# Where the convolution weights and a second image's rows are asked for, and seven early units instead of eight

## The chip, the cores and the metric

One core of one Trainium2 chip. The metric is the device time of one execution in microseconds (us); less is better. The kernel before took 3022.46 us, the median of 3 runs (3018.35 to 3022.87). Everything is float32.

## What is computed

Two layers on x of shape (2, 256, 64, 64). Layer 0: attention over all 4096 pixels with 8 heads of 32 channels, a 1x1 convolution of x and its result, blended with x by a mask. Layer 1: a channel gate, attention in windows of 8 x 8 pixels, and then the part that the change is about:

```
x = x + o                                     # o: window attention
x = channel shuffle in 4 groups
y = conv 7x7, 64 groups of 4 channels -> 64   # sa_w1
y = relu(batch norm 1(y))
y = conv 7x7, 64 groups, 64 -> 256            # sa_w2
return x * sigmoid(batch norm 2(y))
```

## The kernel before

**Stages.** Projections q, k, v of all pixels go to DRAM (to about 187 us of the span). Then one loop over 512 slots (image, chunk of 512 pixels, half of the heads, piece of 128 keys) does layer 0's attention, to about 2781 us. The rest of layer 0 and the window attention of a finished chunk are the steps of a generator (`stage`), laid between the slots. Each chunk ends in a store of 8 image rows into a DRAM tensor `xs` (line 979). The last chunk of image 1 comes through after the loop, between 2784 and 2850 us, so the last rows of image 1 are in `xs` only then. All of image 0 is there much earlier.

**The convolutions** (`convolve`, a generator, from line 992) come last. They are written as matmuls with banded weights: a band covers 30 rows of a padded column block, three blocks make the 64 rows, so a unit of 16 channels (4 groups of 4) for one image is 3 x 64 = 192 moving columns, and for both images 384. There are 16 units. The loop runs over *items*, each a unit and the images it is done for:

```
items = [(u, (0,)) for u in range(EARLY)] + [(u, (1,)) for u in range(2, EARLY)]
items += [(u, (0, 1)) for u in range(EARLY, NU)] + [(1, (1,)), (0, (1,))]
```

With EARLY = 8 that is items 0 to 7 for image 0 (units 0 to 7), items 8 to 13 for image 1 (units 2 to 7), items 14 to 21 for both (units 8 to 15), and 22 and 23, units 1 and 0 of image 1: 24 items. A single item is one without, a pair one with both images.

**One item k.** `conv1` (matmuls on line 1045 into PSUM tile c1a, ReLU by ScalarE on line 1053 into yca), then `conv2` (matmuls on line 1069 into two PSUM tiles c2a, tanh on line 1079 and a scaling on line 1085 by ScalarE into tile za, of which there are two), then `gate` (a product by VectorE on line 1091, and 12 stores for each image to the output, line 1104). In program order conv1 of item k + 1 goes ahead of conv2 of item k. The stores go to the queues of GpSimd (POOL) and SyncE (SP) in turn; those of image 0's items that come after the last chunk is through go to GpSimd alone (line 1096).

**Loads**, all on SyncE's queue, which runs in program order:
- `load_w(u)`, line 1017: one unit's two weight bands, 128 partitions x 1792 values, 896 KB, in the profile wa<-ws. Unit 0 has a buffer of its own; the others take the buffers (8 of them, EB) in which attention kept its exponentials ea, so a first load into one waits until VectorE has added up the exponentials there, and a ninth load waits for the unit that was there before. Units come from a list `weights`: 1 to 15, then 1 again for item 22.
- `load_x(k)`, line 1024: the rows of item k, 128 x 3 x 280 values, 420 KB for each image. Image 0's early items take four buffers xea, later ones four buffers xla. `load_rows(n)` issues these loads up to item n, and stops at items of image 1 until the last chunk is through (`staged`). The first xla loads are then issued by `more()`, four at once; since they read `xs`, they wait until the store of the last rows has landed. For the last chunk two of these four stores are on SyncE's queue and two on GpSimd's.

**Order around the change.** Two weights (units 1 and 2) are asked for at attention's end; after the gate of each of the items 0 to 6 one more; after item 7 none; from item 8 on one per item. After the loop of slots a step of the convolution generator alternates by hand with steps of `stage` for the last chunk (lines 1199 to 1210). SyncE's queue thus holds, from attention's end: w1, w2; stores of item 0, rows of item 4, w3; stores of 1, rows of 5, w4; stores of 2, rows of 6, w5; stores of 3, rows of 7, w6; the store of the last rows; rows of items 8 to 11; w7, w8, w9; stores of item 8, rows of 12, w10; and so on.

TensorE's order there is: conv1 of items 0 and 1, the last chunk's steps with conv1 of item 2 to 5 and conv2 of items 0 to 3 between them, the last projection (line 953, opa), conv2 of item 4, conv1 of 6, conv2 of 5, conv1 of 7, conv2 of 6, conv1 of 8.

Of the kernel before, what the change touches and what calls it, by code (L numbers as in the profile page):

```python
# [29 lines left out]
AHEAD = 2  # L30
EB = 8
DN = 8
EARLY = 8
HEADS1, HD1 = 4, 64
WS = 8
NW = W // WS
# [19 lines left out]
def conv_seq_kernel(ctx: ExitStack, tc: tile.TileContext, a, out):  # L56
# [467 lines left out]
    def pipeline(arm, shifted, pools):  # L524
# [462 lines left out]

        items = [(u, (0,)) for u in range(EARLY)] + [(u, (1,)) for u in range(2, EARLY)]
        items += [(u, (0, 1)) for u in range(EARLY, NU)] + [(1, (1,)), (0, (1,))]
        staged = []  # L990

        def convolve():
# [12 lines left out]
            weights = deque([*range(1, NU), 1])  # L1005
            dst = out.rearrange("b (g i) r w -> b i r g w", i=4)

            def load_w(u):
                if u >= NU:
                    return  # L1010
                n = 2 * 32 * UW
                if u == 0:
                    t = cpool.tile([P, n], F32, name=f"w{arm}{u}")
                else:
                    t = ep.tile([P, HG, CH], F32, tag="e", name=f"w{arm}{u}")
                    t = t.rearrange("p h n -> p (h n)")[:, 0:n]
                nc.sync.dma_start(t, w_s[u])
                ws[u] = t

            def load_x(k):  # L1020
                u, images = items[k]
                x = xs[k] = early[k % 4] if k < EARLY else xcs[k % 4]
                for i, b in enumerate(images):
# [5 lines left out]
            def load_rows(k):  # L1029

                while len(xs) < min(k + 1, len(items)) and (
                    staged or B - 1 not in items[len(xs)][1]
                ):
                    load_x(len(xs))

            def conv1(k):
                if k >= len(items):
                    return
                u, images = items[k]
                n = nb * len(images)  # L1040
                w = ws[u][:, 0 : 32 * UW].rearrange("p (m g d) -> p g d m", g=UG, d=KS)
                s = psum1(f"c1{arm}{k}")
                for d in range(KS):
                    for j in range(4):
                        nc.tensor.matmul(  # L1045
                            s[32 * j : 32 * j + 32, 0 : n * W],
                            w[:, j, d, :],
                            xs[k][:, 0:n, j, d : d + W],
                            start=(d == 0),
                            stop=(d == KS - 1),  # L1050
                        )
                y = ys[k] = ycs[k % 2]
                nc.scalar.activation(
                    y[:, 0:n, PAD : PAD + W],
                    s[:, 0 : n * W].rearrange("p (n x) -> p n x", x=W),
                    AF.Relu,
                    bias=cbias1[:, u : u + 1],
                )

            def conv2(k):  # L1060
                u, images = items[k]
                n = nb * len(images)
                y = ys.pop(k)
                w = ws[u][:, 32 * UW :].rearrange("p (m d) -> p d m", d=KS)
                tiles = [psum2(f"c2{arm}{k}_{hh}") for hh in range(2)]
                for d in range(KS):
                    for j in range(4):
                        r = slice(32 * j, 32 * j + 32)
                        nc.tensor.matmul(  # L1069
                            tiles[j // 2][:, j % 2, 0 : n * W],  # L1070
                            w[r, d],
                            y[r, 0:n, d : d + W],
                            start=(d == 0),
                            stop=(d == KS - 1),
                        )
                z = pool.tile([P, 4, B * nb * W], F32, tag="z", name=f"z{arm}{k}", bufs=2)
                z = z[:, :, 0 : n * W]
                for hh in range(2):
                    nc.scalar.activation(  # L1079
                        z[:, 2 * hh : 2 * hh + 2, :],  # L1080
                        tiles[hh][:, :, 0 : n * W],
                        AF.Tanh,
                        scale=0.5,
                    )
                nc.scalar.activation(z, z, AF.Copy, bias=0.25, scale=0.25)
                return z.rearrange("p j (n x) -> p j n x", x=W)

            def gate(k, z):
                u, images = items[k]
                x = xs[k][:, 0 : nb * len(images), :, PAD : PAD + W]  # L1090
                nc.vector.tensor_mul(z, z, x.rearrange("p n g x -> p g n x"))  # L1091

                engines = (nc.gpsimd, nc.sync)
                if k == len(items) - 1:
                    engines = (nc.scalar, nc.sync)
                elif staged and k < EARLY:
                    engines = (nc.gpsimd,)
                stores = 0
                for m, b in enumerate(images):
                    for n, (x0, r0, r1) in enumerate(BLOCKS):  # L1100
                        for i in range(4):
                            p = 32 * i + 1 - x0
                            stores += 1
                            engines[stores % len(engines)].dma_start(  # L1104
                                dst[b, i, r0:r1, UG * u : UG * u + UG, :],
                                z[p + r0 : p + r1, :, nb * m + n, :],
                            )


            def more():  # L1110
                if staged and not xcs:

                    for n in range(3):
                        t = ep.tile([P, HG, CH], F32, tag="sum", name=f"xl{arm}{n}", bufs=3)
                        t = t.rearrange("p h n -> p (h n)")[:, 0 : B * nb * UG * WP]
                        xcs.append(t.rearrange("p (n g w) -> p n g w", n=B * nb, g=UG, w=WP))
                    xcs.append(pool.tile([P, B * nb, UG, WP], F32, name=f"xl{arm}3"))
                    load_rows(EARLY + 3)
                return bool(xcs)
# [2 lines left out]
            load_rows(3)  # L1122
            load_w(0)
            pool = yield
            for _ in range(2):
                load_w(weights.popleft())
            conv1(0)
            yield
            for k, (u, images) in enumerate(items):
                while len(xs) <= k + 1 < len(items):  # L1130
                    if not more():
                        yield
                conv1(k + 1)
                yield
                more()
                z = conv2(k)
                yield
                more()
                gate(k, z)
                if xcs or k + 4 < EARLY:  # L1140
                    load_rows(k + 4)

                if weights and (k < EARLY - 1 or k >= EARLY):
                    load_w(weights.popleft())

        def run_later():
# [23 lines left out]
        for i, (b, c, g, m) in enumerate(slots):  # L1170
            now[0] = i
            if (b, c, g, m) == (B - 1, NCHUNK - 1, 0, 0):
                for _ in banded:
                    pass
                conv = convolve()
                next(conv)
            if m % PB == 0:
                load_piece(i // PB + AHEAD)
            if g == KC - 1 and m == 0:
                nxt = (b, c + 1) if c + 1 < NCHUNK else (b + 1, 0)  # L1180
                if nxt[0] < B:
                    load_q(*nxt)
            rest = scores(i + 2) if i + 2 < len(slots) else None
            products(i)
            if rest:
                rest()
            if g == KC - 1 and m == NMB - 1:
                at(DN + 6, lambda b=b, c=c: stages.append(stage(b, c)))
            run_later()
            if i % 5 == 1:  # L1190
                next(banded, None)
            if i % 4 == 0:
                run_stages()
# [102 lines left out]
```

## Time and profile before

| | |
|---|---|
| median of 3 runs | 3022.46 us (3018.35 to 3022.87) |
| the profiled execution, its own time | 3021.93 us |
| its span, first to last instruction | 3020.1 us |
| TensorE (PE) busy | 2970.8 us, 98% |
| VectorE (DVE), ScalarE (ACT) busy | 2503.1 us, 2480.6 us |
| GpSimd (POOL) busy | 267.1 us |
| mean granted TensorE clock | 0.993 |

By stretches of the span (us):

| stretch | length | TensorE busy | clock | GB/s |
|---|---|---|---|---|
| attention, 140 to 2781 | 2641.0 | 2630.3 | 1.00 | 76 |
| last chunk and items 0 to 3, 2781.0 to 2847.3 | 66.3 | 61.3 | 0.97 | 101 |
| items 4 to 13, 2847.3 to 2910.2 | 62.9 | 53.4 | 0.92 | 179 |
| pairs and the end, 2910.2 to 3020.1 | 109.9 | 93.9 | 0.93 | 155 |

How to read the lines that follow. Times are from the span's start. A line of a timeline or of the chain has start, length, engine, source line, and output<-inputs of a group of instructions. "SPq" is SyncE's queue, where a DMA's issue stands, not its transfer. "x56" counts the matmul records of a group. In brackets is the time for which the engine was idle before, and what released it. The chain of waits is the work that ended last, followed back from the end.

### The profile page before, as it was taken

How to read it: one execution, taken by the hardware profiler on the slowest of the kernel's cores; microseconds unless marked ns; L12 is line 12 of the kernel's file. 1: busy time of each engine (PE TensorE's matmuls, PEld its weight loads, DVE VectorE, ACT ScalarE, POOL GpSimd, SP SyncE). 2: the span in 40 equal slices, each digit the busy share in tenths (PEclk: the TensorE clock that was granted, in tenths of full speed). 3: DMA queues.
4: the chain of work that ended last, by engine and by line, in shares of the span. 5: the costliest groups of instructions: out<-in, count | busy, mean ns of one | idle time of the engine just before them, and what ended most of it. 6: DMA issues, size and time to landing. Idle time of an engine off the chain costs nothing.

```text
span 3020.1 us, 61026 instructions
## 1 busy us (share of the span) xinstructions
PE 2970.8 (98%) x25226; PEld 1017.2 (34%) x25226; DVE 2503.1 (83%) x1348; ACT 2480.6 (82%) x4151; POOL 267.1 (9%) x470
## 2 busy tenths in 40 slices
PE   9999899999999999999999999999999999999897
PEld 3552223223222222222223222323223222323585
DVE  3249989999999999998999999999999998998211
ACT  5569789898989898988989898989898998988333
POOL 8010000000000000000000000000000000000456
PEclk9999999999999999999999999999999999999998
DMA  8544322222142323232222222222323222321564
GB/s 243 196 174 160 107 69 66 69 65 70 52 80 63 79 62 73 66 73 68 67 68 64 71 58 67 62 73 62 80 59 69 71 71 67 104 60 54 163 196 104
DMA packets 224143, 266.03 MB, mean 88 GB/s; under 512 B 113576, under 2 KB 130300, under 8 KB 223600
## 3 DMA queue, kind: packets, MB, share of 16 engines
q1 hardware_dynamic: 200880, 231.47, 26.2%
q0 software_dynamic: 18416, 27.87, 4.4%
q8 instruction: 201, 3.29, 0.5%
q10 hardware_dynamic: 4560, 2.70, 0.3%
q14 instruction: 86, 0.70, 0.1%
HBM read 213.49 MB, written 66.13 MB: 93 GB/s over the span
## 4 chain that ended last, share of the span: by engine, by line
PE 92%; DVE 2%; DMA 2%; POOL 1%; ACT 1%; issue 1%; SPq 0%; ACTq 0%; DVEq 0%; POOLq 0%
PE sa L633 36%; PE ava L662 33%; PE hya L732 4%; PE qka L803 4%; PE vwa L889 2%; PE opa L953 2%; PE v L472 2%; PE q L435 2%; PE k L435 2%; DVE suma L664 1%; POOL out_dram L1104 1%; PE c1a L1045 1%; PE c2a L1069 1%; DMA out_dram<-za 1%; PE dna L685 1%
## 5 line engine op out<-in xcount | busy, mean ns | idle before, releaser
L664 DVE TENSOR_TENSOR suma<-suma,ea 128x2048 f32<-128x2048 f32 x960 | 2199.1, 2291 | 88.7 <-ACT ea L643 2.3
L643 ACT ACTIVATE ea<-sa 128x512 f32<-128x512 f32 (+1 forms) x3072 | 2044.8, 745 | 86.6 <-PE sa L633 39.3
L633 PE MATMUL sa<-qa,ka 32*128 32x512 f32 x8192 | 1191.4, 640 | 1.5 <-ACT vst L480 1.2
L662 PE MATMUL ava<-ea,va 128*32 128x512 f32 x8192 | 1091.6, 605 | 0.3 <-ACT fa L672 0.3
L633 PEld LDWEIGHTS sa<-qa,ka 32*128 32x128 f32 x8192 | 338.0, 183 | 755.4 <-ACT ea L643 688.3
L662 PEld LDWEIGHTS ava<-ea,va 128*32 128x32 f32 x8192 | 161.5, 108 | 779.7 <-issue 752.9
L979 POOL DMA_DIRECT2D xs<-xo x94 | 65.8, 708 | 2552.0 <-DVE xo L964 2551.8
L1104 POOL DMA_DIRECT2D out_dram<-za x210 | 117.9, 569 | 85.0 <-DVE za L1091 61.1
L803 PE MATMUL qka<-ua,qkv_w 128*128 128x512 f32 x256 | 118.4, 605 | 0.0
L664 DVE TENSOR_TENSOR suma<-ea,ea 128x2048 f32<-128x2048 f32 x32 | 73.1, 2284 | 51.3 <-ACT ea L643 51.3
L1091 DVE TENSOR_TENSOR za<-za,xla 128x768 f32<-128x768 f32 (+1 forms) x16 | 21.7, 1359 | 108.0 <-DMA out_dram<-za 57.9
L454 DVE TENSOR_REDUCE top<-sq 128x512 f32<-128x2048 f32 x16 | 36.6, 2286 | 81.3 <-ACT sq L448 81.3
L1069 PE MATMUL c2a<-yca,wa 32*128 32x192 f32 (+1 forms) x1344 | 98.1, 435 | 2.5 <-ACT za L1079 2.5
L740 ACT ACTIVATE ta<-hya,bf 128x512 f32<-128x512 f32 x32 | 20.2, 683 | 96.8 <-PE hya L732 96.8
L1079 ACT ACTIVATE za<-c2a 128x384 f32<-128x384 f32 (+1 forms) x48 | 26.1, 595 | 86.5 <-DMA out_dram<-za 61.4
L1069 PEld LDWEIGHTS c2a<-yca,wa 32*128 32x128 f32 x1344 | 89.6, 315 | 13.1 <-issue 9.8
L858 ACT ACTIVATE ewa<-ewa,mxwa 128x64 f32<-128x64 f32 x256 | 85.2, 346 | 1.5 <-DVE mxwa L849 1.5
L744 DVE TENSOR_TENSOR ta<-ta,mca 128x512 f32<-128x512 f32 x32 | 22.0, 689 | 67.6 <-ACT ta L740 67.6
L816 ACT ACTIVATE qka<-qka,qkv_b 128x512 f32<-128x512 f32 x64 | 40.4, 683 | 41.8 <-PE qka L803 41.6
L803 PEld LDWEIGHTS qka<-ua,qkv_w 128*128 128x128 f32 x256 | 46.0, 189 | 71.3 <-issue 46.1
L435 PE MATMUL q<-x,WqT 128*128 128x512 f32 x128 | 61.3, 624 | 5.6 <-DMA WqT<-in_WqT_dram 5.6
L889 PE MATMUL vwa<-qkv_w,ua 128*128 128x256 f32 x256 | 59.5, 386 | 0.0
(137 smaller groups left out, 1523.5 us busy)
## 6 DMA issues: line engine op xcount, KB each, us to landing
ka<-ks SPq DMA_DIRECT2D x256, 256.0 KB
va<-vs SPq DMA_DIRECT2D x256, 256.0 KB
wa<-ws SPq DMA_DIRECT2D x17, 896.0 KB
ws<-zeros SPq DMA_DIRECT2D x16, 896.0 KB
xs<-xo POOLq DMA_DIRECT2D x78, 140.0 KB, 5.8
xla<-xs SPq DMA_DIRECT2D x24, 420.0 KB
x<-in_x_dram SPq DMA_DIRECT2D x16, 512.0 KB
qs<-qst SPq DMA_DIRECT2D x16, 512.0 KB
```

The lines of the kernel that those rows point to most:

```text
L435: nc.tensor.matmul(s[:, g, :], w[:, kc, g * P : (g + 1) * P], rhs, start=(kc == 0), stop=(kc == KC - 1),)
L633: nc.tensor.matmul(heads[j], k[r, cols], q[r, g, :], start=True, stop=not shifted)
L643: nc.scalar.activation(e[:, h, :], tile, AF.Exp, scale=SCALE0)
L662: nc.tensor.matmul(av[r, :], v[:, m % PB, r], e[:, j, :], start=start, stop=stop)
L664: nc.vector.tensor_add(total, first[0] if m == 1 else total, e)
L732: nc.tensor.matmul(s[:, oc, :], wf[:, kc, oc * P : (oc + 1) * P], f[:, kc - KC, :] if half else xw[kc], start=(kc == 0), stop=(kc == 2 * K ...
L803: nc.tensor.matmul(s[:, j, :], wqkv[:, kc, o : o + P], u[:, kc, :], start=(kc == 0), stop=(kc == KC - 1),)
L858: nc.scalar.activation(e[:, n, :], e[:, n, :], AF.Exp, bias=mx[:, n : n + 1], accum_out=rs[:, n : n + 1],)
L889: nc.tensor.matmul(sv[:, t, :], u[:, kc, t * P : (t + 1) * P], wqkv[:, kc, 2 * C : 3 * C], start=(kc == 0), stop=(kc == KC - 1),)
L979: eng.dma_start(x_s[b, n, p + r0 : p + r1].rearrange("r g w -> g r w"), xo[64 * h : 64 * h + 64, oc, r0 - WS * c : r1 - WS * c, :],)
L1069: nc.tensor.matmul(tiles[j // 2][:, j % 2, 0 : n * W], w[r, d], y[r, 0:n, d : d + W], start=(d == 0), stop=(d == KS - 1),)
L1104: engines[stores % len(engines)].dma_start(dst[b, i, r0:r1, UG * u : UG * u + UG, :], z[p + r0 : p + r1, :, nb * m + n, :],)
```

## The change

Three lines. EARLY goes from 8 to 7: units 0 to 6 are done for image 0 first, units 2 to 6 for image 1 after that, and units 7 to 15 are pairs; 23 items. At attention's end four weights are asked for instead of two. And the rule for the others changes: one after each gate as long as the next in the list is unit 9 or less (1 + EB), and from item EARLY on.

```diff
-EARLY = 8
+EARLY = 7
...
             pool = yield
-            for _ in range(2):
+            for _ in range(4):
                 load_w(weights.popleft())
             conv1(0)
...
                 if xcs or k + 4 < EARLY:
                     load_rows(k + 4)
 
-                if weights and (k < EARLY - 1 or k >= EARLY):
+                if weights and (weights[0] <= 1 + EB or k >= EARLY):
                     load_w(weights.popleft())
```

SyncE's queue then holds: w1, w2, w3, w4; stores of item 0, rows of item 4, w5; stores of 1, rows of 5, w6; stores of 2, rows of 6, w7; stores of 3, w8; the store of the last rows; rows of items 7 to 10; w9; stores of item 7, rows of 11, w10; stores of 8, rows of 12 (the first pair), w11; and so on. TensorE's order is the same up to conv2 of item 5; conv1 of item 7 behind it is unit 2 of image 1, on the first xla rows, where it was unit 7 of image 0.

## The prediction

> **What bounds the kernel now.** I read the page first: TensorE is busy for 98% of the span, nearly all of it in attention, which the change leaves alone. So I went to the end of the trace, in this order: the chain of waits, TensorE's and SyncE's timelines, short windows with the granted clock. An "item" is one turn of the convolution loop; w3 is unit 3's weights; "rows" are the loads into xea and xla.
>
> The chain of waits (start, length, what) has two weight loads and one store of image 1's rows in it:
>
> ```profile
> 2809.24 5.58 DMA wa<-ws
> 2814.86 2.53 PE c1a L1045 x56
> ...
> 2849.74 6.23 DMA xs<-xo
> 2856.16 0.38 SPq L1024
> 2856.59 0.50 SPq L1024
> 2857.14 0.48 SPq L1024
> 2857.66 0.51 SPq L1024
> 2858.22 7.80 DMA wa<-ws
> 2866.15 4.62 PE c1a L1045 x55
> ```
>
> TensorE's timeline (start, length, group, idle before it and releaser) gives the three stalls, at items 3, 5 and 7:
>
> ```profile
> 2814.86 2.53 PE L1045 MATMUL c1a<-xea,wa 128*32 128x192 f32 x56 [1.24 <-DMA wa<-ws]
> ...
> 2839.46 4.19 PE L1045 MATMUL c1a<-xea,wa 128*32 128x192 f32 x56 [1.84 <-DMA wa<-ws]
> ...
> 2866.15 4.62 PE L1045 MATMUL c1a<-xea,wa 128*32 128x192 f32 x56 [9.38 <-DMA wa<-ws]
> 2870.70 3.58 PE L1069 MATMUL c2a<-yca,wa 32*128 32x192 f32 x56
> 2874.20 2.54 PE L1045 MATMUL c1a<-xla,wa 128*32 128x192 f32 x56
> ```
>
> Two of these conv1 groups take 4.19 and 4.62 us where an undisturbed one takes 2.54. SyncE's timeline says why item 7 waits: w7, w8 and w9 are asked for behind four loads of rows, and these behind the landing of the store of the last rows (2848.76).
>
> ```profile
> 2848.76 1.33 SPq L979 DMA_DIRECT2D xs<-xo  x2
> 2856.16 2.01 SPq L1024 DMA_DIRECT2D xla<-xs  x4
> 2858.22 1.54 SPq L1017 DMA_DIRECT2D wa<-ws  x3
> ```
>
> The windows (the last three columns: granted clock, DMA share, GB/s) give the reason for the slow groups:
>
> ```profile
> 2839.40:2843.60 4.20, 4.14 (x57) 3.50 (x57) 0.00 (x0) 0.06 (x1) 3.37 (x6) 0.59 0.28 55
> ...
> 2866.00:2868.00 2.00, 1.85 (x24) 1.38 (x28) 0.00 (x0) 0.00 (x0) 1.40 (x4) 0.50 1.05 425
> ```
>
> From 2874.20 on TensorE is busy without a gap worth naming until 2999.7 (118.22 of 118.3 us in 2876.7 to 2995.0): TensorE bounds that stretch. The stalls ahead of it are waits for DMA.
>
> **What the Trainium skill says.** *TensorE: Matmul & The Clock Gate*, section "Part 1: The HAM clock gate (the "warmup" mystery)": the array falls to half clock after an idle window and comes back after a busy one, about 3.4 us each, and the windows run freely. The trace agrees: half-microsecond windows show the clock fall at about 2839.7 and 2860.2 and rise at 2843.2 and 2870.5, all on one grid of 3.41 us. 1.24 us idle did not make it fall, 1.84 us did. *DMA: Bandwidth & Descriptors*, section "Queues, rings and completion order": on each DMA engine a ring's descriptors are consumed in order. It agrees: w7 landed at 2866.02, when about 3.2 MB had moved (2.64 MB of them the four row loads and w7), not at 2870.4 when w8 and w9 were through too. Same page, "Two DMAs through the same engine are not ordered": a load of what an earlier DMA stores must wait for that DMA's completion. So the rows wait for the store's landing, 2849.74 + 6.23 = 2855.97, and the change cannot remove that.
>
> **The change, part by part.** I take the span of the profiled execution, 3020.1 us, inside its own time, 3021.93.
>
> *w3 and w4 at attention's end.* They move on SyncE's queue from behind the stores of items 0 and 1 to straight after w2. Their buffers are those of the last exponentials, freed by VectorE's sums (2.38 us each, the last ending at 2784.3), so they are issued at about 2772.4 and 2774.8 where w1 and w2 were at 2767.6 and 2770.0. This is a new wait on SyncE; the next thing behind it is item 0's stores at 2805.02, 30 us later, and DMA is idle there, so it costs 0. Item 3 no longer waits: **1.24 us**.
>
> *w5 to w8 one by one.* Item 0 asks for w5 where it asked for w3 (2809.24), and so on; w8 takes w6's place at item 3. At item 5 w5 has been in place for 20 us. The 1.84 us of waiting go and the clock stays up, 4.19 - 2.54 = 1.65. What is late next there is the last projection (opa): with all shifted 1.24 earlier its inputs are ready at 2838.2, conv1 ends at 2838.85. So opa starts at 2838.85 instead of 2843.58: **3.49** more, 4.73 in all.
>
> *Seven units.* Item 7 is now unit 2 of image 1, and needs rows instead of w7. All up to the store of the last rows follows opa, so the store is issued 4.73 earlier, at 2844.03. w8 (896 KB) is asked for at about 2842.1 and moves until 2846.3, sharing the engines with that store: I add 0.3, so it lands at 2851.5. The first load of rows goes out at 2851.7. Its landing is not in the trace, since nobody waited for it. Bounds: it is first in the ring, 0.43 MB; 3.3 us, because by 2859.0 the windows had moved 0.48 MB since 2857.0, its 0.43 among them, and I add 0.5 for the landing (2859.5, against an issue at 2856.16); or, if the four loads end together, 7.6 us. I take 3.3, because of the order in the ring: 2855.0. TensorE ends item 5's conv2 at 2856.78 - 4.73 = 2852.05, so it **waits 3.0 us** where it waited 9.38. The clock will fall: 3.0 us split over two windows of 3.41 leaves at least 1.5 in one. Its price is 1.65 and 2.08 in the two cases seen; I take 1.8, bounds 0 and 2.1. Stall before 9.38 + 2.08 = 11.46, after 4.8: **6.7 us** less. w9 stays behind the rows, but is used only at item 14.
>
> *Unit 7 in one item.* It was two single items, each 2.47 + 3.50 = 5.97 us of TensorE (start to start, 2874.20 to 2880.18); it is now one pair, 9.63 (2928.04 to 2937.69). TensorE bounds this stretch, so **2.3 us** less. Of the rest, 24 stores to the output stay 24, and 12 of them go from GpSimd alone to both queues; ScalarE does 3.6 us for the pair instead of 4.3, hidden beside 9.63; one row load of 0.43 MB at 2843.36 goes away, its image comes with the pair.
>
> What could be late next: the rows of the first pair, item 12. They are asked for after item 8's gate, which waits for item 6's twelve stores on GpSimd (0.58 us each, 7 us). I put item 6's gate at 2865.6, its stores' end at 2872.6 and landing near 2875.2, item 8's gate at 2878.2, and the pair's rows 7.85 later (as from 2902.3 to 2910.17 now): 2886.1, where conv1 of item 12 is due at 2886.8. It just fits; bounds 0 and 1.5 us, I take 0.
>
> Sum: 1.24 + 3.49 + 6.7 + 2.3 = 13.7. 3021.93 - 13.7 = **3008.2 us**. The median of the runs shown is 3022.46, 0.5 above that execution; I let the number stand.
>
> **The rivals.**
> *The stall is only renamed.* The four row loads end together at 7.6 us: rows at 2859.3, wait 7.3, clock 2.1, so 4.6 more than above: 3012.8. For it: they are issued within 2.01 us. Against it: w7's landing ahead of w8 and w9.
> *The gain is paid back at the first pairs.* z buffers and stores run late, and items 12 and 13 each wait 2.5 us and lose the clock, 1.8: 8.6 back, 3016.8, within 0.2% of before. For it: ScalarE starts on the results of items 9 and 10 0.9 and 1.4 us late for such stores now (2893.06, 2899.58). Against it: item 7's stores are now shared by SyncE, so GpSimd's backlog is smaller.
> *Slower: the loads of items 8 to 11 become DMA-bound.* Each such item of 5.97 us of TensorE has to move rows for a pair (0.86 MB), weights (0.92) and stores (0.26): 2.04 MB, 342 GB/s. At 250 GB/s each takes 8.2, 2.2 late, with 1.8 for the clock 4.0, four times 16: 3024.2. It decides below 269 GB/s, where 1.6 + 1.8 four times make up 13.7. For it: the DMA share is mostly near 1.0 from 2907 to 2920. Against it: the kernel has four such items already and TensorE waits 0.08 us in them.
> *The change doesn't do what it says:* the program's order shows w5 to w8 ahead of the last rows' store and w9 behind the rows, so no weights are left ahead of a waiting item; nothing for this.
>
> **How the numbers follow.** Likeliest case 0.81, ends together 0.11, paid back 0.05, slower 0.03. The likeliest case's own range: no clock loss 3006.4; rows 1 us early as well 3005.4; 1.5 us late at the pair and a full clock loss 3010.0; and runs of one kernel lie up to 4 us under their median, 3004. With the first rival the range is 3004 to 3013.5. A measurement here can tell about 0.2%, 6 us, from no change. Faster by over that: the first two cases, 0.92; within it 0.05; slower 0.03.
>
> **What would show it.** In the profile after: no idle ahead of conv1 of items 3 and 5, and 2.5 us for each; one wait of 2 to 4 us for xla ahead of item 7, about 2852 to 2855, with the clock at 0.5 behind it; nine pairs of 9.63 us, the first at about 2887; a span near 3006. It is wrong if the wait ahead of item 7 is over 5 us, if TensorE idles before items 12 to 15, or if the store of the last rows isn't issued near 2844.

## The result, and the profile after

The changed kernel takes **3008.72 us** (median of 5 runs, 3007.0 to 3010.86); the kernel before, run beside it, 3022.46 us (5 runs, 3018.35 to 3024.31). The ratio is 0.9956, with a 95% interval of 0.9942 to 0.9971: 13.7 us less, where 13.7 had been worked out and 3008.2 us predicted. The profiled execution took 3007.63 us; its span is 3005.7 us where it was 3020.1, its mean granted clock 0.996 where it was 0.993.

The first view is TensorE's timeline of the kernel after (start, length, group, and in brackets the idle time before it and its releaser): conv1 of items 0, 3 and 5, the last projection, conv2 of item 4, conv1 of item 7, conv2 of item 6, conv1 of item 8, the first pair, and the last conv2.

```profile
2780.27 0.37 PE L1045 MATMUL c1a<-xea,wa 128*32 128x192 f32 x3
2813.02 2.53 PE L1045 MATMUL c1a<-xea,wa 128*32 128x192 f32 x56
2835.68 2.54 PE L1045 MATMUL c1a<-xea,wa 128*32 128x192 f32 x56
2838.15 3.70 PE L953 MATMUL opa<-ota,out_w 128*128 128x512 f32 x8
...
2847.76 3.57 PE L1069 MATMUL c2a<-yca,wa 32*128 32x192 f32 x56
...
2855.17 3.87 PE L1045 MATMUL c1a<-xla,wa 128*32 128x192 f32 x56 [3.84 <-DMA xla<-xs]
2858.97 3.64 PE L1069 MATMUL c2a<-yca,wa 32*128 32x192 f32 x56
2862.55 2.54 PE L1045 MATMUL c1a<-xla,wa 128*32 128x192 f32 x56
...
2886.45 4.81 PE L1045 MATMUL c1a<-xla,wa 128*32 128x384 f32 x56
...
2986.12 3.56 PE L1069 MATMUL c2a<-yca,wa 32*128 32x192 f32 x52 [0.47 <-ACT za L1079]
```

Of the three stalls the first two are gone: items 3 and 5 have no bracket, and their conv1 takes 2.53 and 2.54 us. At item 7 a wait of 3.84 us for rows stands where 9.38 us for weights stood. The first pair starts without a wait.

SyncE's queue of the kernel after, from the same stretch: the four weights at attention's end, w8, its two stores of the last rows, the four loads of rows, w9.

```profile
2767.07 7.49 SPq L1017 DMA_DIRECT2D wa<-ws  x4
...
2839.97 0.37 SPq L1017 DMA_DIRECT2D wa<-ws  x1
2843.33 1.33 SPq L979 DMA_DIRECT2D xs<-xo  x2
2851.52 1.99 SPq L1024 DMA_DIRECT2D xla<-xs  x4
2853.62 0.52 SPq L1017 DMA_DIRECT2D wa<-ws  x1
```

Half-microsecond windows of the same stretch (length, busy time of TensorE, of its weight loads, of VectorE, ScalarE and GpSimd, then granted clock, DMA share, GB/s) show that w8's bytes, asked for at 2839.97, are nearly through when the store's begin:

```profile
2843.50:2844.00 0.50, 0.50 (x13) 0.50 (x12) 0.40 (x1) 0.00 (x0) 0.41 (x1) 1.00 0.89 363
2844.00:2844.50 0.50, 0.50 (x14) 0.50 (x12) 0.00 (x0) 0.00 (x0) 0.50 (x2) 1.00 0.24 80
```

Only one weight load is left behind the rows. The rows are issued 8.19 us after the store was (2851.52 - 2843.33), and TensorE goes on 3.65 us after that (2855.17 - 2851.52).

Windows of the kernel after around that start (the same columns):

```profile
2853.00:2856.20 3.20, 1.03 (x25) 1.06 (x29) 0.96 (x1) 0.10 (x1) 3.20 (x6) 1.00 1.01 338
2856.20:2859.70 3.50, 3.50 (x48) 2.69 (x41) 0.00 (x0) 0.42 (x1) 2.80 (x6) 0.52 1.07 407
2859.70:2862.00 2.30, 2.30 (x46) 2.30 (x44) 0.00 (x0) 0.00 (x0) 0.99 (x2) 1.00 0.44 162
```

The clock is still full when conv1 starts and then half for about 3.5 us. From conv1 of item 7 to conv1 of item 8 it is 7.38 us where 5.97 is undisturbed: 1.41 us lost.

GpSimd's end of the kernel before, and then of the kernel after:

```profile
2998.82 11.37 POOL L1104 DMA_DIRECT2D out_dram<-za  x20 [2.22 <-issue]
```

```profile
2984.38 2.19 POOL L1104 DMA_DIRECT2D out_dram<-za  x4 [0.62 <-DVE za L1091]
2989.25 7.91 POOL L1104 DMA_DIRECT2D out_dram<-za  x14 [2.67 <-issue]
```

Fourteen stores come after 2.67 us in which GpSimd waits for nothing that the profile shows ("issue"); in the kernel before twenty stores came after 2.22 such us. The experiments come back to it. In the kernel before the last conv2 also waited longer, where it now waits 0.47 us:

```profile
3002.21 4.40 PE L1069 MATMUL c2a<-yca,wa 32*128 32x192 f32 x52 [2.51 <-ACT za L1079]
```

**Where the 14.4 us of span went.** Each row is the distance between two starts on TensorE in the two traces:

| stretch | before | after | less | predicted |
|---|---|---|---|---|
| to the first conv1 (attention's end) | 2780.79 | 2780.27 | 0.52 | 0 |
| to conv1 of item 3 | 34.07 | 32.75 | 1.32 | 1.24 |
| to the last projection | 28.72 | 25.13 | 3.59 | 3.49 |
| to conv1 of item 8 | 30.62 | 24.40 | 6.22 | 6.7 |
| to the end of the span | 145.90 | 143.15 | 2.75 | 2.3 |
| sum | | | 14.40 | 13.7 |

### The profile page after: what moved, and what is told of

It reads as the page before. It is cut to its first block, busy times and chain, and to the rows that moved or that the text cites. A ratio compares the mean times of both kernels' runs of the same rounds, so it can differ in the third digit from the quotient of the medians.

```text
span 3005.7 us, 60793 instructions
## 1 busy us (share of the span) xinstructions
PE 2964.7 (99%) x25114; PEld 1010.5 (34%) x25114; DVE 2502.0 (83%) x1347; ACT 2479.9 (83%) x4147; POOL 263.7 (9%) x464
## 4 chain that ended last, share of the span: by engine, by line
PE 91%; DMA 3%; DVE 2%; POOL 1%; ACT 1%; issue 1%; SPq 0%; ACTq 0%; DVEq 0%; POOLq 0%
PE sa L633 36%; PE ava L662 33%; PE qka L803 4%; PE hya L732 4%; PE vwa L889 2%; PE opa L953 2%; PE v L472 2%; PE q L435 2%; PE k L435 2%; POOL out_dram L1104 1%; DVE suma L664 1%; DMA wa<-ws 1%; DMA out_dram<-za 1%; PE dna L685 1%; PE sca L837 1%
## 5 line engine op out<-in xcount | busy, mean ns | idle before, releaser
L1091 DVE TENSOR_TENSOR za<-za,xla 128x1536 f32<-128x1536 f32 (+1 forms) x16 | 22.5, 1409 | 110.9 <-ACT za L1085 61.6
L1045 PE MATMUL c1a<-xla,wa 128*32 128x384 f32 (+1 forms) x896 | 62.5, 429 | 3.8 <-DMA xla<-xs 3.8
```

What stands on the lines that cost most here:

```text
L1045: nc.tensor.matmul(s[32 * j : 32 * j + 32, 0 : n * W], w[:, j, d, :], xs[k][:, 0:n, j, d : d + W], start=(d == 0), stop=(d == KS - 1),)
```

## The experiments

The theory is that of the prediction: two weight waits go at once, the third is replaced by a wait for the landing of the last rows' store and the first load behind it, and one unit fewer is split. All are medians of at least five runs, beside the kernel before on the same chip: 3021.97 us there with the weights alone, seven units alone, six weights at the end and w9 first; 3023.03 with rows last, six units, the fill and eight units with shared stores; 3022.15 and 3021.93 with the last two pairs of runs.

**One part alone: the weights' places with eight units** (the kernel after, but)

```diff
-EARLY = 7
+EARLY = 8
```

> The changed kernel with EARLY back at 8: only the weights' requests are changed. My theory: w7 is there, so conv1 of item 7 (unit 7 of image 0) runs at once and covers the landing of image 1's rows, which item 8 needs 6 us later. The stalls of items 3, 5 and 7 all go: 4.9 us at opa as in the changed kernel, then 11.5 us at item 7; unit 7 costs 2.3 us more as two items. Against the changed kernel, whose item 7 loses 3.84 of waiting and 1.41 to the clock: 5.25 - 2.3 = 2.9 us faster, about 3005.8. Rival: four items whose stores go to GpSimd alone (48 stores of 0.58 us, 28 us, while TensorE needs 24) run late, the z buffers come free late and TensorE waits 1 to 3 us in items 7 to 10: 3007 to 3009, no better than the changed kernel. A second rival, that the early weights bring nothing without the seven units: 3022.

Measured: 3010.73 us (3008.73 to 3011.12), ratio 0.9961 (0.9947 to 0.9974). The first rival was right in kind, and the loss was larger than its 1 to 3 us. Item 7, unit 7 of image 0, does cover the rows: neither it nor item 8 waits. But TensorE's timeline of this run has other lines:

```profile
2860.71 4.29 PE L1069 MATMUL c2a<-yca,wa 32*128 32x192 f32 x56
...
2879.34 0.78 PE L1069 MATMUL c2a<-yca,wa 32*128 32x192 f32 x4
2882.50 4.87 PE L1069 MATMUL c2a<-yca,wa 32*128 32x192 f32 x52 [2.38 <-ACT za L1079]
2887.30 3.13 PE L1045 MATMUL c1a<-xla,wa 128*32 128x192 f32 x56
```

conv2 of item 7 takes 4.29 us instead of 3.57, and conv2 of item 10 stands for 2.38 us and then runs at a lower clock: from conv1 of item 8 to that of item 14 5.2 us more than in the run with shared stores below. ScalarE could not take item 9's results there: they go into the za of item 7, whose stores had not left it. All stores of items 4 to 7 go through GpSimd, which has 23 in a row without a rest. ScalarE's wait for za, and these stores:

```profile
2881.96 0.87 ACT L1079 ACTIVATE za<-c2a 128x384 f32<-128x384 f32 x2 [7.70 <-DMA out_dram<-za]
```

```profile
2863.03 12.74 POOL L1104 DMA_DIRECT2D out_dram<-za  x23 [0.24 <-DMA out_dram<-za]
```

So the rival of the prediction that saw a loss from late stores named a true mechanism. With seven units item 7 is image 1 and its stores are shared, and the loss does not come.

**The other part alone: seven units with the weights where they were** (the kernel before with EARLY = 7)

```diff
-EARLY = 8
+EARLY = 7
```

> The kernel before with EARLY = 7 alone: two weights at attention's end and the old rule. My theory: items 3 and 5 wait for w3 and w5 as before (1.24, and 1.84 with 1.65 for the clock), but item 7 no longer needs w7, so it waits for the rows only, as in the changed kernel. 4.9 us slower than the changed kernel: 3013.6, and 8.8 faster than before. Rival: the gain of the change comes from the early weights alone, and the seven units give nothing but the packed item (2.3 us): 3020.

Measured: 3012.04 us (3009.19 to 3013.44), ratio 0.9965 (0.9953 to 0.9977). The rival is out, and the median 1.6 below the number expected. The waits at items 3 and 5 are there, 1.35 and 1.79 us, and at item 7 3.04 us for rows. One thing that had been put higher is in TensorE's timeline of this run at item 5:

```profile
2839.97 2.55 PE L1045 MATMUL c1a<-xea,wa 128*32 128x192 f32 x56 [1.79 <-DMA wa<-ws]
```

The same wait that cost the kernel before 4.19 - 2.54 = 1.65 us of clock costs nothing here. This is no full account of the 1.6: the profiled execution itself took 3013.09 us, only 0.5 below the number, because item 7 lost 2.36 us to the clock instead of 1.41, and the end after the last conv2 was 17.2 us long instead of 16.0.

**Six weights at attention's end** (the kernel after, but)

```diff
-            for _ in range(4):
+            for _ in range(6):
```

> The changed kernel with six weights asked for at attention's end instead of four, so that w7, w8 and w9 follow at items 0 to 2 and nothing is asked for between item 3's stores and the store of the last rows. In the changed kernel that store landed 8.19 us after SyncE issued it, before 7.40. Theory: w8, still moving when the store is issued, makes the 0.8 us; here the landing takes 7.4 us or less, the wait ahead of item 7 is about 3.0 us, and the time is 0.8 us less, about 3007.9. Rival: the landing of that store varies by itself, and the wait stays 3.8 us, 3008.7.

Measured: 3008.21 us (3007.76 to 3008.8), ratio 0.9955 (0.9941 to 0.9968). The rows go out 7.47 us after the store and item 7 waits 2.96 us, about as expected. The total does not tell it from the kernel after, since the clock cost 2.34 us here instead of 1.41. And the landing is no proof either: with w8 in its place it took 8.19, 7.73, 8.01, 7.39, 7.53 and 8.31 us in six runs with seven units, and 7.50, 8.84 and 7.83 us with eight and six units, so 7.47 lies within the scatter.

**w9 ahead of the rows** (the kernel after, in `more()`)

```diff
+                    load_w(weights.popleft())
                     load_rows(EARLY + 3)
```

> The changed kernel with w9 asked for just ahead of the four loads of rows instead of just behind them. Theory: what item 7 waits for is the first load in the rings, so 0.92 MB ahead of it at 350 to 400 GB/s add 2.3 to 2.6 us to the wait, 6.1 to 6.4 us in all, and the clock costs 1.4 to 2.1: 2.3 to 3.3 us slower, about 3011.5. Rival: the loads share the engines evenly and end together, so their order doesn't matter: no difference, 3008.7, wait 3.8 us.

Measured: 3010.07 us (3009.32 to 3011.65), ratio 0.9962 (0.9949 to 0.9976). The wait was not 6.1 to 6.4 but 4.25 us, 2.19 of clock behind it. SyncE's queue of this run shows the mistake:

```profile
2844.39 1.33 SPq L979 DMA_DIRECT2D xs<-xo  x2
2845.81 1.13 SPq L1017 DMA_DIRECT2D wa<-ws  x1
2852.55 1.97 SPq L1024 DMA_DIRECT2D xla<-xs  x4
```

w9 waits for nothing, so SyncE issued it at 2845.81, and it moved while the store was landing. It does not stand between the landing and the rows, and the run is no test of the order in the ring.

**Item 7's rows last of the four** does test that order (the kernel after, in `more()`):

```diff
-                    load_rows(EARLY + 3)
+                    for k in (EARLY + 1, EARLY + 2, EARLY + 3, EARLY):
+                        load_x(k)
```

> The changed kernel with the four first loads of rows in another order: items 8, 9, 10, and then item 7, the one that TensorE waits for. Unlike w9, which waits for nothing and moved while the store of the rows was landing, these three loads cannot start before it either. Theory: the rings take the loads in order, so 1.29 MB at 350 to 400 GB/s stand ahead, 3.2 to 3.7 us more of waiting (7.0 to 7.5 in all) and a clock loss of about 2: 3012 to 3013. Rival: the loads share the engines evenly and all end at once, at 7.6 us, in either order: 3008.7 and a wait of 3.8.

Measured: 3014.48 us (3012.62 to 3015.82, 7 runs), ratio 0.9971 (0.9960 to 0.9982). TensorE's timeline of this run:

```profile
2860.88 4.71 PE L1045 MATMUL c1a<-xla,wa 128*32 128x192 f32 x56 [7.26 <-DMA xla<-xs]
```

The rows were issued at 2853.17 and the last landed 7.7 us later, where as first it takes 3.5 to 4.1. So the load issued first is usable about 4 us before the one issued last; the two between were not timed. The prediction's first rival, all four ending together, is out. The time is about 2 us above the expected 3012 to 3013; wait and clock (2.41) came as expected, but attention ended at 2782.54 in this execution, 2.27 later than in the kernel after, which is no part of the edit.

**Six units** (the kernel after, but)

```diff
-EARLY = 7
+EARLY = 6
```

> The changed kernel with EARLY = 6: one item of image 0 less ahead of the rows, units 6 to 15 as pairs. Theory: what TensorE can do before the rows land shrinks by one item, 5.97 us, so the wait ahead of item 6 is about 9.8 us and the clock costs 2.1, against 3.84 and 1.41; the extra pair saves 2.3: 4.4 us slower than the changed kernel, about 3013. Rival: the packing of units into pairs is what brings the gain of seven over eight, and six bring as much again: 3006.5.

Measured: 3012.96 us (3012.45 to 3015.01), ratio 0.9967 (0.9955 to 0.9979); the wait for rows is 9.46 us and 2.36 of clock follow. One item fewer ahead of the rows was expected to be 5.97 us more of waiting and is 5.62 by these two traces; one split unit fewer gives back 2.3.

**TensorE busy while it waits** (the kernel after, and three matmuls more ahead of conv1 of item 7, into a PSUM tile that nobody reads: work that the reference does not have)

```diff
+                if k + 1 == EARLY:
+                    s = psum2(f"fill{arm}")
+                    for _ in range(3):
+                        nc.tensor.matmul(
+                            s[:, 0, :], ident, wqkv[:, 0, 0:CH], start=True, stop=True
+                        )
                 conv1(k + 1)
```

> The changed kernel with three matmuls of 128x512 (about 0.9 us each, their result is never read) between conv2 of item 5 and conv1 of item 7, where TensorE waits for the rows. They add work that isn't in the reference and change no output. Theory: the 1.4 to 2.3 us lost behind the wait are the clock's; with TensorE idle for only about 1 us the clock stays up, conv1 takes 2.5 us, and the time is 1.4 to 2.3 us less, about 3007. Rival: conv1 is slow there because the rows and w9 are being written to SBUF at 380 GB/s at the same time; no change, 3008.7.

Measured: 3008.16 us (3007.03 to 3008.74), ratio 0.9950 (0.9936 to 0.9963). TensorE's timeline and a window of this run:

```profile
2853.23 2.84 PE L1136 MATMUL filla<-qkv_w,ident 128*128 128x512 f32 x6
2857.24 2.54 PE L1045 MATMUL c1a<-xla,wa 128*32 128x192 f32 x56 [1.17 <-DMA xla<-xs]
```

```profile
2857.20:2859.80 2.60, 2.56 (x60) 2.31 (x60) 0.00 (x0) 0.00 (x0) 2.22 (x4) 1.00 1.06 376
```

The wait for rows is as long (2.84 of it filled), but the clock stays at 1.00 and conv1 takes 2.54 us, although 376 GB/s move beside it. So the 1.41 us of the kernel after are the clock, not contention. From the last projection to conv1 of item 8 it is 23.10 us instead of 24.40; the median gains 0.6 of these 1.3, and that is within the scatter.

**Eight units, stores shared** (the kernel after, but)

```diff
-EARLY = 7
+EARLY = 8
...
-                elif staged and k < EARLY:
+                elif staged and k < EARLY - 3:
                     engines = (nc.gpsimd,)
```

so that only item 4's stores go through GpSimd alone.

> Eight units and the early weights, as in the run with the weights alone, but GpSimd alone takes only item 4's stores; those of items 5, 6 and 7 go to GpSimd and SyncE in turn. In that run TensorE lost 0.73 us in conv2 of item 7, 4.45 in conv2 of item 10 and 0.59 behind it, each time because ScalarE waited for output stores before it could free PSUM. Theory: GpSimd's backlog is the cause; with the stores shared these 5.8 us go and item 7 still covers the landing of the rows, so about 3005, some 4 us faster than the changed kernel. Rival: the stores are late because the DMA engines are full with row loads and weights, whoever issues them; then it stays near 3010.

Measured: **3004.18 us** (3003.51 to 3005.16), ratio 0.9939 (0.9925 to 0.9952): the fastest of all, 4.5 below the kernel after. TensorE's timeline of this run has no idle time ahead of a group there. One short loss for stores is left: conv2 of item 7 takes 4.08 us instead of 3.57, because ScalarE gets za for item 6 only when item 4's stores, still GpSimd's alone, have left it (second view):

```profile
2857.97 2.55 PE L1045 MATMUL c1a<-xla,wa 128*32 128x192 f32 x56
2860.44 4.08 PE L1069 MATMUL c2a<-yca,wa 32*128 32x192 f32 x56
2864.45 2.55 PE L1045 MATMUL c1a<-xla,wa 128*32 128x192 f32 x56
```

```profile
2860.42 0.87 ACT L1079 ACTIVATE za<-c2a 128x384 f32<-128x384 f32 x2 [5.41 <-DMA out_dram<-za]
```

From conv1 of item 8 to that of item 14 it is 36.37 us, against 41.59 in the first experiment. With the stores shared, an eighth unit of image 0 covers the store and load through `xs`. Whether that is worth more than the 2.3 us of the pair, the next run has to tell.

**Seven units, stores shared** (the kernel after, with `k < 5` for `k < EARLY` in that line) and **the kernel before, stores shared** (the same edit there) ask whether sharing helps by itself.

> The changed kernel, and GpSimd alone takes only item 4's stores; those of items 5 and 6 are shared with SyncE. It tells whether the gain of the run with eight units and shared stores comes from the sharing by itself. Theory: with seven units TensorE never waited for an output store between items 6 and 12, so the sharing brings nothing: 3008.7, within 1 us, and the wait ahead of item 7 stays at 3 to 4 us. Rival: sharing is worth 4 to 6 us in either form: 3003 to 3005.

> The kernel before with the shared stores of items 5, 6 and 7 alone, weights and units as they were. Theory: its 11.5 us at item 7 gave GpSimd time to catch up, and no wait of TensorE was for a store, so no change: 3022, within 2 us. Rival: GpSimd's backlog cost the kernel before something too, up to the 5.8 us seen with the weights alone: 3016 to 3020.

Measured: 3004.82 us (3003.14 to 3008.23), ratio 0.9945 (0.9932 to 0.9959), and 3018.97 us (3016.16 to 3023.68, 13 runs), ratio 0.9991 (0.9983 to 1.0). Both medians are over 3 us lower than I had expected, where the rivals had put them; for the kernel before the interval reaches 1.0, so its gain is not clear of noise. And seven units with shared stores are only 0.6 us from eight, with ranges that overlap: that an eighth unit is better than seven once the stores are shared is not shown. For the first, TensorE's timeline and GpSimd's end:

```profile
2855.10 2.55 PE L1045 MATMUL c1a<-xla,wa 128*32 128x192 f32 x56 [3.30 <-DMA xla<-xs]
```

```profile
2994.95 1.19 POOL L1104 DMA_DIRECT2D out_dram<-za  x2 [2.64 <-issue]
```

Two things are new. The wait of 3.30 us cost no clock this time, so from the last projection to conv1 of item 12 it is 46.35 us instead of 48.30. And GpSimd's unexplained gap stands ahead of its last 2 stores instead of 14: from the last conv2's end to the end of the span it is 14.4 us instead of 16.0. Of the kernel before with shared stores the same holds at the end (2 stores behind the gap instead of 20, and its last conv2 waits 0.18 us instead of 2.51); its item 5 also lost nothing to the clock. This left open whether the gap moved because of which stores were shared.

**Other stores taken from GpSimd** (the kernel after; items 0 and 1 store through SyncE, items 4 to 6 as they did), and **the kernel after once more** beside it:

```diff
                     engines = (nc.gpsimd,)
+                elif k < 2:
+                    engines = (nc.sync,)
```

> The changed kernel with the output stores of items 0 and 1 all issued by SyncE (twelve fewer for GpSimd, as in the run that shares the stores of items 5 and 6), while items 4 to 6 stay with GpSimd alone. Theory: GpSimd's idle stretch near the end stands at a fixed number of its DMAs, whichever stores they are. Then it moves behind all but the last two stores, the time from the last conv2's end to the span's end is 14.4 us instead of 16.0, and the median is about 1.6 less, 3007.1 us. Rival: the shorter end came from sharing the stores of items 5 and 6 itself; then the end stays at 16.0 us with 14 stores behind the idle stretch, and the median at 3008.7 us.

> The changed kernel as it is, once more, beside the others: 3008.7 us within 1. The wait of item 7's conv1 for its rows is 3.8 us within 0.5. If the loss to the clock depends on how the wait falls on free-running windows, it may come out anywhere from 0 to 2.4 us at the same wait, and attention's end anywhere from 2780.3 to 2783.0; if it is fixed by the program, it is 1.4 us again.

Measured: 3007.67 us (3007.17 to 3009.22), ratio 0.9952 (0.9938 to 0.9965), and 3009.48 us (3008.98 to 3011.13), ratio 0.9958 (0.9944 to 0.9971): 1.8 apart, as the theory had it. So the end accounts for about 1.8 of the 3.9 us by which the medians of seven units with shared stores and the kernel after differ. In the profiled executions the rest is item 7's clock (1.41) and a wait shorter by 0.54; whether that holds for the other four executions stays open. GpSimd's end with items 0 and 1 on SyncE, and then of the repeat:

```profile
2986.01 8.91 POOL L1106 DMA_DIRECT2D out_dram<-za  x16 [0.62 <-DVE za L1091]
2997.02 1.19 POOL L1106 DMA_DIRECT2D out_dram<-za  x2 [2.10 <-issue]
```

```profile
2985.93 2.20 POOL L1104 DMA_DIRECT2D out_dram<-za  x4 [0.61 <-DVE za L1091]
2990.79 7.94 POOL L1104 DMA_DIRECT2D out_dram<-za  x14 [2.66 <-issue]
```

Stores of quite another time were taken away, and the gap moved by the same twelve. From the last conv2's end to the span's end it is 14.2 us, in the repeat 16.2. The page's count says it exactly: GpSimd has 470 instructions in the kernel before, 464 after and 452 in the four runs that take stores from it; 20, 14 and 2 of them come after the gap, so it always stands behind the first 450. With six units it is 458, and 8 come after. There the end is 16.1 us, no shorter than with 14: the chain of waits still runs from the gap through six stores on GpSimd to the last product. With 2 behind the gap the last product has started before the gap ends (2996.52 against 2997.02 with items 0 and 1 on SyncE).

The repeat also bears on the clock. TensorE's timeline of it, conv1 of items 7 and 8:

```profile
2855.88 4.71 PE L1045 MATMUL c1a<-xla,wa 128*32 128x192 f32 x56 [3.54 <-DMA xla<-xs]
...
2864.14 2.55 PE L1045 MATMUL c1a<-xla,wa 128*32 128x192 f32 x56
```

The same program waits 3.54 us and then loses 8.26 - 5.97 = 2.29 us, where it lost 1.41 after 3.84 before. Its span is 1.8 longer than that of the first profiled execution: 0.95 of that is attention's end (2781.22 instead of 2780.27), 0.88 the clock.

## Why the prediction was right, step by step

- **w3 and w4 at attention's end, 1.24 us**: 1.32 by the traces. SyncE's four loads stand there for 7.49 us and nobody is behind them until the stores of item 0, as was said. With the weights in their old places (second experiment) the wait is 1.35.
- **w5 to w8 one by one, 3.49 us**: 3.59 by the traces. Both terms were there, the wait and the clock. The second one had luck in it: it was the loss of that one profiled execution, and two other runs with the same wait, 1.79 and 1.86 us, lost nothing (seven units alone; the kernel before with shared stores). On another execution of the kernel before this step could have been worth 1.8 us.
- **The last part's stall, 6.7 us**: 6.22. Its mechanism held, its terms were off a little. The landing took 8.19 us after the issue, not 7.7 (7.40 and 0.3 for w8); the first rows came 3.65 us after their issue, not 3.3. Together 0.84, which is the wait of 3.84 instead of 3.0. The clock's price was 1.41, not 1.8. That the first load is first to land is shown by the run with item 7's rows last. Whether w8 beside the store lengthens the landing, as I had argued with the 0.3, stays open: 7.4 to 8.8 us with w8 there, 7.47 without. It had little to share in the kernel after: w8 was asked for at 2839.97, not at about 2842.1, and was through by about 2844.3, not 2846.3.
- **Unit 7 as a pair, 2.3 us**: the stretch gave 2.75. A pair is 9.64 us, from one start to the next, and two single items 5.97 each, so 2.30 is the pair. Most of the other 0.45 is the end: the last conv2 waits 0.47 us at full clock where it waited 2.51 and lost 0.83 to the clock, and then the end after it is 16.0 us long where it was 13.5. The prediction had put nothing for the end. That 14 stores, not 20, come after GpSimd's gap there is not shown to matter.
- **Nothing late at the first pair**: conv1 of item 12 started at 2886.45 without a wait; due by the prediction at 2886.8. The rival of late stores is real with one more item through GpSimd alone, as the first experiment shows, and the reason given against it, that item 7's stores are now shared, is what keeps it away.
- **"The clock will fall" after 3.0 us** was put too strongly. With seven units and item 7's rows first, it fell in six of seven traces in which that item waited (2.96 to 4.25 us, the filled one apart), and not in one (3.30 us). The bound of 0 for it was right.

The size also agrees with the medians: 13.74. That it does so to a tenth is luck: the repeat's median is 0.8 higher, those of the kernel before lie between 3021.93 and 3023.03, and the sum holds two prices of the clock, 1.65 and 1.8, that other executions paid as 0 or as 2.3. That attention ended 0.52 us earlier in the profiled execution is no part of the change: across the runs it ends between 2780.3 and 2783.0.

## What to carry to other kernels

Put the loads that need no fresh data ahead of a wait in an in-order queue, and count what is left behind that wait: here weights behind one store's landing had cost a stall of 11.5 us with its clock. Cover a store and load through DRAM, some 11.8 us from issue to use here (8.19 and 3.65), with work that needs neither side of it; an eighth unit does that, once its stores do not crowd one queue, though it did not come out clearly faster than seven with the same sharing. When a stall is priced, price the clock behind it as a range from one profile, since the same program lost 1.4 and 2.3 us there.

## What the runs showed of the hardware that I had not expected

**The clock's price differs for like waits.** Wait ahead of a conv1, and what that item then lost (for item 5 conv1's time less 2.54, else the time to the next item's conv1 less 5.97):

| run | wait (us) | lost (us) |
|---|---|---|
| before, item 5 | 1.84 | 1.65 |
| seven units alone, item 5 | 1.79 | 0 |
| before with shared stores, item 5 | 1.86 | 0 |
| seven units, shared stores, item 7 | 3.30 | 0 |
| six weights at the end, item 7 | 2.96 | 2.34 |
| seven units alone, item 7 | 3.04 | 2.36 |
| after, item 7 | 3.84 | 1.41 |
| after once more, item 7 | 3.54 | 2.29 |
| items 0 and 1 on SyncE, item 7 | 3.77 | 2.19 |
| w9 first, item 7 | 4.25 | 2.19 |
| rows last, item 7 | 7.26 | 2.41 |
| before, item 7 | 9.38 | 2.08 |
| six units, item 6 | 9.46 | 2.36 |

The Trainium skill (*TensorE: Matmul & The Clock Gate*, section "Part 1: The HAM clock gate (the "warmup" mystery)") says that the windows run freely, and the traces agree: within each execution the falls and rises of the granted clock lie on one grid of 3.41 us, and from execution to execution the grid lies elsewhere. This gives the two prices of the one program. In the kernel after's first trace the clock fell at about 2856.2, when conv1 had run for 1.0 us, and was back one window later. In the repeat it fell at about 2854.5, during the wait, and was back two windows later (the same columns as in the windows above):

```profile
2853.00:2854.40 1.40, 0.00 (x0) 0.00 (x0) 0.26 (x1) 1.08 (x2) 1.40 (x3) 1.00 0.88 186
2854.50:2861.30 6.80, 5.42 (x64) 3.66 (x68) 0.60 (x1) 0.42 (x1) 5.55 (x10) 0.50 1.04 384
2861.40:2863.40 2.00, 2.00 (x44) 2.00 (x37) 0.00 (x0) 0.00 (x0) 1.68 (x3) 1.00 0.13 33
```

It also speaks of at least one idle window, about 3.4 us, before the clock falls; here 1.84 us was enough, and the measurement decides. How busy a window must be to keep the clock up stays open. The wait of 3.30 us that cost nothing lay across a step of its grid (counted back from the fall after the last matmul), and TensorE was busy for 59% and 44% of the two windows; with six weights at attention's end the clock fell after a window that was busy for 50%. So the share of busy time alone does not decide it. That the phase makes the difference is read from executions as they came; no run set it.

**GpSimd's gap.** 2.1 to 2.7 us in which GpSimd waits for nothing that the profile shows, always after its 450th instruction, in all fourteen traces. Counted in its DMAs that is the 418th, and a shorter pause of the same kind, 0.6 to 1.7 us, stands after the 297th in all fourteen. In the kernel after:

```profile
2880.97 1.71 POOL L1104 DMA_DIRECT2D out_dram<-za  x3 [1.65 <-issue]
```

What happens there stays open. With seven units, twelve fewer stores on GpSimd put it behind all but two, and the span's end is 1.6 to 2.0 us nearer to the last conv2.
